# A two-layer graph-attention kernel: VectorE's order beside seven products of each head, and the rows of layer 2's logits in four column groups

## The chip, the cores and the metric

One core of a Trainium2 chip runs the whole computation in one launch. The metric is the time of an execution on the device in microseconds: 633.06 us before the change, the median of three runs (632.86 to 633.64).

## What is computed

A residual block around a graph network: `x` is 512 nodes by 768 features, with 16,896 directed edges (8192 drawn pairs in both directions, and one loop for each node). Two layers of graph attention follow one another, the first with 8 heads of 768 features each, whose outputs are concatenated, the second with one head.

```python
def gat_layer(x, W, a_s, a_d, b, edge_index, concat):
    h = (x @ W).reshape(n, H, C)
    alpha_s = einsum('nhc,hc->nh', h, a_s)
    alpha_d = einsum('nhc,hc->nh', h, a_d)
    e = leaky_relu(alpha_s[src] + alpha_d[dst], 0.2)
    ...  # softmax of e over the edges that end in one node: alpha
    out = segment_sum(h[src] * alpha[:, :, None], dst, num_segments=n)
    return out.reshape(n, H * C) + b

h = elu(gat_layer(x, W1, a_src1, a_dst1, b1, edge_index, True))    # 512 x 6144
x = layernorm(x + gat_layer(h, W2, a_src2, a_dst2, b2, edge_index, True))
```

All products are in fp32.

## The kernel before

**Stages.** The edges are turned into a dense 512x512 matrix of counts, so the attention of a head is a dense softmax and a product of a 512x512 matrix with the head's 512x768 features. Heads are worked one after the other, and three matrix products make up the work of TensorE for each head `h`: `mixed` (the attention product with the ELU that follows; it writes `gT`, the head's output, transposed), then the head's share of layer 2's product, `second` (512x768 by 768x768, added up in `h2` over the heads), then the projection of head `h + 2` (512x768 by 768x768, into `hs`). While TensorE does these, VectorE (DVE), ScalarE (ACT) and GpSimd (POOL) empty its banks, work the softmax of head `h + 1` and make the operand sums that the fast schemes below need. The loop over `h` runs for 0 to 6; head 0 and the projections of the first heads are by halves, heads 1 to 5 by thirds. Head 7 and layer 2's own attention are written out behind the loop: `last_mixed`, the last `second`, the rows of layer 2's logits, the softmax, the final product and the layernorm.

**Fast products.** By halves, a product is split 2x2 and done in 7 products instead of 8; by thirds, 512x768x768 is split into 2x3 and 3x3 blocks and done in 15 products instead of 18, named `P0` to `P14`. The left operands of some are sums of blocks (`gsums` for `second`; `in_second`, `late_` and `XB` for the projection: the X sums, L1073 and L1076), and so are the right ones (weight sums, L170: `sums` for the projection, `sums2` for `second` of the next head). Each product by thirds is 8 passes of TensorE over 256 columns (L480). It is added into one of five chains, each a bank of PSUM (the pool `mm` has five): `STEPS` gives each product its chain and the block of the output that its bank's present value is added to, or subtracted from. The next product of a chain adds to the same bank, so it must wait until the bank has been read. This reading is the product's "emptying": on DVE by L493, on ACT by L486 for the first value of a block, or on ACT with an adding DMA of POOL (L490, L491). By halves the emptyings are L447 to L451.

For the projection the order of the products is P8, P13, P9, P2, P4, P12, P6, P0, P1, P10, P5, P14, P11, P7, P3 (n = 0 to 14). P14 (n=11) and P7 (n=13) are in one chain, P11 (n=12) and P3 (n=14) in another.

**The order of each engine is written by hand.** Every engine runs its instructions in program order, and the program is a list of closures: product n is issued, then the pieces of work that a table gives to n, then the emptying of n:

```python
for n in range(15):
    pairs[n][0]()            # product n on TensorE
    ...                      # sums, logits, softmax pieces dealt to n, on DVE
    pairs[n][1]()            # emptying of n
```

What the tables deal out, as far as the change touches it: `sums3`, the operand sums of the next head's attention product (`left_sums`, L928 to L931, and `right_sums`, L939 to L942); `half_logits` and `logits` (L418, L424: a product of one tile of features with `a_s` or `a_d`, summed along the row, some 1 us each, four tiles of two for each head); `score`, `scored` and `rank` (the softmax of a tile, L640 to L662); and `sums2`.

**Weights.** `load_second(h + 1)` fetches the next head's layer-2 weights while a projection runs: SP's queue loads the rows in chunks (L145), and POOL's queue adds further blocks into some of them by DMA (`add_up`, L133). `P14`'s block is one of these: rows chunk 2, and then `add_up(B_["P14"], part(0, 1))`, 256 KB, as the second L133 into `w1r` of each head. From it and from `P4`'s block DVE makes `P6 = P14 - P4`, then `P4 = P13 + P4` in place; `P2 = P12 - P13` is made from two other loaded blocks. P2, P6 and P4 are the right operands of products 1, 6 and 3 of `second`.

**Head 0** does `second` by halves: pairs of products with emptyings `e0` and `e1`, and the softmax of head 1's tiles (`scored`) between.

**The tail.** `last_mixed` takes a table of DVE pieces, keyed by a chunk c of the product (0 to 2) and a place in it. `rows` is a bank of PSUM that collects the logits of layer 2 for all nodes in rows: `add_rows` (L1384) multiplies a stationary of 2 columns (`V`, or `al2`, each with a source and a target vector) in one of the array's column groups `j` of 32, so that the result lies on partitions 32j and 32j + 1. `rows` is cleared by a memset beforehand (L1394), copied to `row2`, and `pick` (L1416, L1418) adds the groups up by products with `picks`.

Of the kernel before, what the change touches and what calls it, by code (L numbers as in the profile page):

```python
# [37 lines left out]
def gat_pass(  # L38
# [16 lines left out]
    nc = tc.nc  # L55
    P = 128
# [365 lines left out]
    def logits(h, feats, t):  # L422
        for al, a, sign in zip(AL[h], A[h], (1.0, -1.0)):
            nc.vector.scalar_tensor_tensor(scr, feats[:, t, :], sign, a, op0=ALU.mult,  # L424
                                           op1=ALU.mult, accum_out=al[:, t:t + 1])
# [745 lines left out]
    for h in range(H - 1):  # L1171
# [14 lines left out]
        if h == 0:  # L1186
            GA, gsums = left(gT, gS)
            finish = mixed(0, AA, BB, [[besides[:1], [besides[1], sources[0]]], [[sources[1]], [sources[2]] + row],
                                       [besides[2:], list(targets)]])
            load_w1(2)()  # L1190
            load_a(2, a_src1[2], a_dst1[2])
            attend = attended(0)
            pairs = by_halves(h2, GA, B2)
            for m, _ in pairs[:2]:
                m()
            pairs[0][1]()
            for f in finish:
                f()
            gsums[0]()
            pairs[1][1]()  # L1200
            gsums[1]()
            pending[0]()
            pairs[2][0]()
            gsums[2]()
            pairs[3][0]()
            gsums[3]()
            pending[1]()
            pairs[2][1]()
            pairs[3][1]()
            fold_count(0)  # L1210
            score(0)
            for n in range(2, 7):
                (m0, e0), (m1, e1) = pairs[2 * n:2 * n + 2]
                m0()
                m1()
                if n < 6:
                    scored(n - 2)
                if n < 5:
                    score(n - 1)
                if n == 6:  # L1220
                    turn_in(0)
                    out_by_dma(2)
                e0()
                if 3 < n < 6:
                    out_by_dma(n - 4)
                if n == 6:
                    out_by_dma(3)
                    B2, sums2, load_pairs, load_first, load_rest = load_second(1)
                    load_pairs()
                    load_first()  # L1230
                    load_rest()
                e1()
                if n < 5:
                    fold_count(n - 1)
        else:
            G, gsums = g_thirds(h)

            def of_b(*names):
                return [sums2.pop(p) for p in names if p in sums2]

            amid = [[], of_b("P6", "P2"), behind] if h == 1 else [of_b("P1"), [], of_b("P4")]
            finish = mixed(h, AA, BB, [[[sources[0]], [sources[1]] + amid[0]], [row, [targets[0]] + amid[1]], [amid[2], [targets[1]]]],
                           [gsums[p] for p in ("P13", "P8")])
            behind = []
            if not last:
                load_a(h + 2, a_src1[h + 2], a_dst1[h + 2])
                attend = attended(h)
            pairs = second_by_thirds(h, G, B2)

            def sum_up(*names):  # L1250
                return [gsums[p] for p in names]

            def at(f, *args):
                return [lambda: f(*args)]

            third_sum = of_b("P3")
            plan = {0: of_b("P6") + sum_up("P14") + finish[:1], 1: finish[1:] + of_b("P4") + sum_up("P12"), 2: sum_up("P9", "P7"),
                    3: sum_up("P1") + at(score, 0), 4: sum_up("P6"), 5: at(scored, 0) + at(score, 1), 6: of_b("P1") + sum_up("P10"),
                    7: at(scored, 1) + at(score, 2), 8: sum_up("P5") + third_sum, 9: at(scored, 2) + at(score, 3),
                    10: sum_up("P11"), 11: at(scored, 3), 12: [], 13: sum_up("P3")}  # L1260
            if h > 1:
                plan[0][1:1] = [plan[13].pop()]
            if last:
                plan = {0: finish[:1], 1: finish[1:] + sum_up("P12") + at(score, 0), 2: sum_up("P9", "P7"), 3: sum_up("P1"),
                        4: sum_up("P6") + at(scored, 0) + at(score, 1), 5: sum_up("P14"), 6: sum_up("P10") + at(scored, 1) + at(score, 2),
                        7: at(out_by_dma, 0) + sum_up("P5"), 8: sum_up("P11") + at(scored, 2) + at(score, 3), 9: at(out_by_dma, 1),
                        10: at(scored, 3), 11: at(scale, 2) + sum_up("P3"), 12: third_sum + at(turn_in, 0) + at(scale, 3), 13: at(turn_in, 1)}
                AA, lsums = left_sums(H - 1, pass_.rearrange("p j n -> p (j n)"))
                plan[13] += lsums[:2]
                plan[14] = lsums[2:3]  # L1270
            behind_it = {1: of_b("P7")}

            def also(n, *what):
                plan[n] = plan.get(n, []) + list(what)

            for n, f in zip((8, 10), in_second):
                also(n, f)
            if not last:
                for f in attend:
                    also(13, f)  # L1280
            for n, (multiply, empty) in enumerate(pairs):
                if last and n > 12:
                    turn(q[n - 11], n - 11)
                multiply()
                for f in plan.get(n, []):
                    f()
                empty()
                if not last and n == 13:
                    turn_in(0)
                for f in behind_it.get(n, []):  # L1290
                    f()
                if last:
                    continue
                if n in (7, 9, 11, 14):
                    out_by_dma(min(n - 7, 6) // 2)
                if n == 5:
                    B2, sums2, load_pairs, load_first, load_rest = load_second(h + 1)
                    load_pairs()
                if n == 14:
                    rest_of_thirds()  # L1300
                    reload_x()
                    load_first()
                    load_rest()
        in_second = []
        if 0 < h and not last:
            pairs = project_by_thirds(h + 2, XB, B3)
            AA, sums3 = left_sums(h + 1)
            for n in range(15):
                pairs[n][0]()
                for p in {0: ("P6", "P2"), 1: ("P4",), 4: ("P10",), 5: ("P0",), 6: ("P1",), 9: ("P7",),  # L1310
                          12: ("P3",)}.get(n, ()):
                    sums[p]()
                if n == 5:
                    BB, rsums_ = right_sums()
                    sums3 += rsums_
                if n in (2, 3, 5, 6, 8, 9, 10):
                    for _ in range(2 if n == 8 else 1):
                        sums3.pop(0)()
                if n in (11, 13):
                    logits(h + 2, HS[h + 2], 2 + (n - 11) // 2)  # L1320
                if n in in_third:
                    in_third.pop(n)()
                if n in (12, 14):
                    sums2.pop("P2" if n == 12 else "P6")()
                pairs[n][1]()
                if n in (1, 2, 4):
                    turn_in((n + 2) // 2)
# [55 lines left out]
    def add_rows(lhsT, rhs, j, cols, start, stop):  # L1383
        nc.tensor.matmul(rows[32 * j:32 * j + 2, cols], lhsT, rhs, start=start, stop=stop,  # L1384
                         tile_position=(0, 32 * j), skip_group_check=True)
# [5 lines left out]

    first, second_, third_, fourth = (given(t) for t in range(NT))
    BB, rsums = right_sums()
    finish = last_mixed(AA, BB, [*rsums, lsums[3]], {(1, 0): [lambda: nc.vector.memset(rows, 0.0)], (2, 0): second_[:1], (2, 1): first})  # L1394
    every = slice(0, N)
    pairs = second(GA, B2)

# [2 lines left out]
            f()  # L1400

    run(pairs[0][0], pairs[0][1], pairs[1][0], pairs[1][1], *finish, gsums[0], gsums[1], pairs[2][0], pairs[2][1])
    for c in range(DC):
        add_rows(V[:, c, :], gT[:, c, :], c % 3, every, c < 3, c > 2 and c % 3 != 2)
    run(second_[1], pairs[3][0], gsums[2], pairs[3][1], *third_, pairs[4][0], *fourth, pairs[5][0], pairs[4][1], pairs[5][1], gsums[3],
        pairs[6][0])
    for t in range(NT):
        add_rows(al2[:, :, t], ident, 2, slice(t * P, (t + 1) * P), False, t == NT - 1)
    row2 = work.tile([P, N], F32, name="nr")
    nc.scalar.copy(row2, rows[:, :N])  # L1410
    fold(parts[:2])
# [114 lines left out]
```

## Time and profile before

The profiled execution took 633.37 us, 0.31 above the median; its span, from the first to the last instruction, is 631.6 us.

| | before |
|---|---|
| median of 3 runs | 633.06 us |
| profiled execution | 633.37 us |
| its span | 631.6 us |
| granted TensorE clock | 0.996 |
| TensorE (PE) busy | 620.3 us, 98% |
| TensorE's weight loads (PEld) | 483.1 us, 76% |
| VectorE (DVE) | 529.3 us, 84% |
| ScalarE (ACT) | 336.7 us, 53% |
| GpSimd (POOL) | 149.2 us, 24% |
| TensorE's share of the chain that ended last | 88% |

Weight loads run beside matmuls, and matmuls are pipelined, so a busy time is longer than the distance between starts. In lines of the timeline the columns are the start in us, the length in us, the engine, the line, the operation, output and inputs, their shapes, how many instructions are joined, and in brackets the idle time of the engine just before them with what ended it. In lines of the waits they are who waited for whom, us in total, times, and the longest.

### The profile page before, as it was taken

The numbers are of one execution on the slowest core, as the hardware profiler recorded it, in microseconds if no ns is written. First come the engines' busy times: TensorE is split into PE (matmuls) and PEld (weight loads), VectorE is DVE, ScalarE is ACT, GpSimd is POOL, SyncE is SP. The second block draws the span as 40 slices with busy tenths as digits, with TensorE's granted clock in tenths as the row PEclk, the third lists the DMA queues.
The fourth block names the chain that finished last, engine by engine and source line by source line (L and its number), as shares of the span: only waits on it lengthen the run. The fifth ranks groups of instructions, "written<-read, shape, count | busy, mean of one in ns | idle before, by whom it ended". The sixth has DMA issues, their size and how long they took to land.

```text
span 631.6 us, 8545 instructions
## 1 busy us (share of the span) xinstructions
PE 620.3 (98%) x2761; PEld 483.1 (76%) x2761; DVE 529.3 (84%) x1129; ACT 336.7 (53%) x598; POOL 149.2 (24%) x177
## 2 busy tenths in 40 slices
PE   8999999999999999999999999999999999999995
PEld 5555576556888888888888888888888888885553
DVE  8979989888898889968898778968897878968685
ACT  5875776650658236651658146751758146754361
POOL 1300011023333224323342422323342413010000
PEclk9999999999999999999999999999999999999998
DMA  8994397789999998999999998999999994590042
GB/s 292 329 245 96 70 259 249 173 244 258 246 205 152 320 253 186 181 271 222 254 214 179 310 251 182 187 290 224 226 213 202 304 279 88 124 249 2 17 76 78
DMA packets 109568, 129.45 MB, mean 205 GB/s; under 512 B 41622, under 2 KB 90446, under 8 KB 108750
## 3 DMA queue, kind: packets, MB, share of 16 engines
q1 hardware_dynamic: 75518, 91.35, 47.2%
q0 software_dynamic: 33568, 36.90, 37.7%
q10 hardware_dynamic: 432, 0.59, 0.3%
q8 instruction: 24, 0.39, 0.3%
q14 instruction: 26, 0.21, 0.1%
HBM read 99.84 MB, written 2.90 MB: 163 GB/s over the span
## 4 chain that ended last, share of the span: by engine, by line
PE 88%; DVE 5%; DMA 4%; ACT 1%; issue 1%; SPq 1%; DVEq 0%; POOLq 0%; ACTq 0%
PE mm L480 42%; PE mm L966 17%; PE mm L409 17%; PE mm L1472 3%; DMA w2r<-in_L_gnn_W_dram 3%; PE mm L1008 3%; PE held L409 2%; PE tr L742 1%; DMA w2t<-in_L_gnn_a_dst_dram 1%; PE bc L276 1%; PE held L608 1%; PE bc L742 1%; DVE h L493 0%; PE tr L1384 0%; DVE q L645 0%
## 5 line engine op out<-in xcount | busy, mean ns | idle before, releaser
L486 ACT ACTIVATE hs<-mm 128x512 f32<-128x512 f32 x30 | 17.9, 596 | 89.3 <-PE mm L480 71.2
L966 PE MATMUL mm<-PT,hs 128*128 128x256 f32 x252 | 61.3, 379 | 0.0
L493 DVE TENSOR_TENSOR hs<-hs,mm 128x512 f32<-128x512 f32 x45 | 30.8, 685 | 27.6 <-PE mm L480 27.6
L966 PEld LDWEIGHTS mm<-PT,hs 128*128 128x128 f32 x252 | 47.8, 190 | 7.2 <-ACT u L970 0.3
L649 ACT ACTIVATE q<-q,nmax 128x512 f32<-128x512 f32 x32 | 23.1, 721 | 52.9 <-DVE nmax L645 52.8
L491 POOL DMA_DIRECT2D h<-pass x22 | 26.5, 1319 | 84.4 <-ACT pass L490 75.5
L493 DVE TENSOR_TENSOR h<-h,mm 128x512 f32<-128x512 f32 x56 | 38.3, 684 | 6.2 <-PE mm L480 5.7
L966 PE MATMUL mm<-pS,gS 128*128 128x256 f32 x168 | 43.1, 379 | 0.0
L903 ACT COPY PT<-zr 128x1024 uint16<-128x1024 uint16 x34 | 39.2, 1155 | 1.5 <-DMA zr<-pS 0.9
L480 PE MATMUL mm<-w2r,gT 128*128 128x256 f32 x160 | 37.9, 385 | 0.0
L480 PE MATMUL mm<-w2r,xT 128*128 128x256 f32 x160 | 37.8, 379 | 0.0
L133 POOL DMA_DIRECT2D w1t<-in_L_gnn_W_dram x18 | 29.4, 1658 | 29.5 <-DMA w1t<-in_L_gnn_W_dram 28.7
L966 PEld LDWEIGHTS mm<-pS,gS 128*128 128x128 f32 x168 | 31.9, 190 | 4.3
L480 PE MATMUL mm<-w1t,hs 128*128 128x256 f32 x144 | 34.2, 380 | 0.5 <-DVE h L493 0.5
L480 PEld LDWEIGHTS mm<-w2r,gT 128*128 128x128 f32 x160 | 29.6, 190 | 6.6 <-DVE hs L493 3.0
L480 PE MATMUL mm<-w1r,gS 128*128 128x256 f32 x144 | 34.0, 379 | 0.0
L480 PE MATMUL mm<-w1r,hs 128*128 128x256 f32 x144 | 34.0, 379 | 0.0
L480 PEld LDWEIGHTS mm<-w2r,xT 128*128 128x128 f32 x160 | 30.4, 190 | 4.1
L970 ACT COPY u<-mm 128x256 f32<-128x256 f32 x21 | 7.8, 371 | 45.7 <-PE mm L966 45.7
L480 PEld LDWEIGHTS mm<-w1t,hs 128*128 128x128 f32 x144 | 27.2, 190 | 4.7 <-DVE h L493 0.9
L716 DVE TENSOR_SCALAR os<-nodes,idx 128x512 bf16<-128x512 f16 x104 | 29.2, 355 | 1.4 <-PE tr L742 1.4
L480 PEld LDWEIGHTS mm<-w1r,gS 128*128 128x128 f32 x144 | 27.3, 190 | 3.7
(295 smaller groups left out, 1566.6 us busy)
## 6 DMA issues: line engine op xcount, KB each, us to landing
w2r<-in_L_gnn_W_dram SPq DMA_DIRECT2D x48, 384.0 KB
w1r<-in_L_gnn_W_dram SPq DMA_DIRECT2D x43, 384.0 KB
gT<-xd SPq DMA_DIRECT2D x5, 1280.0 KB
w1t<-in_L_gnn_W_dram SPq DMA_DIRECT2D x24, 256.0 KB
h<-pass POOLq DMA_DIRECT2D x22, 256.0 KB, 4.3
w1t<-in_L_gnn_W_dram POOLq DMA_DIRECT2D x18, 256.0 KB, 6.0
w2t<-in_L_gnn_W_dram SPq DMA_DIRECT2D x15, 256.0 KB
w2t<-in_L_gnn_W_dram POOLq DMA_DIRECT2D x15, 256.0 KB, 8.9
```

The source lines that it names most:

```text
L133: nc.gpsimd.dma_start(o, i, accum_op=ALU.add)
L409: nc.tensor.matmul(ps[:, :HALF], A_[p][:, k, i * P:(i + 1) * P], B_[p][:, k, :], start=start and k == 0, stop=k == HK - 1, skip_group_chec ...
L480: nc.tensor.matmul(bank[chain][:, i * TH:(i + 1) * TH], A_[p][:, k, i * P:(i + 1) * P], B_[p][:, k, :], start=first and i == k == 0, stop= ...
L486: nc.scalar.activation(out(o), ps, AF.Copy, scale=sign)
L491: nc.gpsimd.dma_start(out(o), part, accum_op=ALU.add)
L493: nc.vector.tensor_tensor(out(o), out(o), ps, op=ALU.add if sign > 0 else ALU.subtract)
L649: nc.scalar.activation(q, q, AF.Exp, bias=nmax, scale=-1.0, accum_out=dens[t])
L716: nc.vector.tensor_scalar(o, nodes, idx[:, c:c + 1], None, op0=ALU.is_equal)
L903: nc.scalar.copy(PT.rearrange("p s n -> p (s n)").bitcast(U16).rearrange("p (s n h) -> p s n h", s=NT, h=2)[:, :, t * P:(t + 1) * P, :], p ...
L966: nc.tensor.matmul(bank[p][:, :HN], A_[p][:, k, c * P:(c + 1) * P], B_[p][:, k, :], start=over is None and k == 0, stop=k == 1, skip_group ...
L1008: nc.tensor.matmul(banks[c, p][:, :HN], A_[p][:, k, c * P:(c + 1) * P], B_[p][:, k, :], start=over is None and k == 0, stop=k == 1, skip_g ...
L1472: nc.tensor.matmul(ps[:, :cols.stop - cols.start], PT[:, s, t * P:(t + 1) * P], h2[:, s, cols], start=(s == 2), stop=(s == 1))
```

## The change

It has five parts. (1) Head 0, n=3: the emptying `e0` goes ahead of `scored(1)`. (2) `in_second`, two X sums beside `second` of head 1: from products 8 and 10 to 12 and 14. (3) The projection loop (heads 1 to 5): DVE's sums and logits are dealt to other products; P7 and P3 of the projection's weight sums one and two products earlier; the four logits of tiles 2 and 3 to n = 11, 13, 14, 14 instead of two at 11 and two at 13; of `sums2`, P2 from n=12 to n=4, P6 from n=14 to n=12, and P4 from the next attention product (`amid`) to n=14. (4) The tail: the memset of `rows` ahead of `last_mixed`, one logit from (2, 0) to (1, 1). (5) The rows: `V`'s six products of 512 columns, two in each of three groups, become four of 512 columns, one in each of four groups, and four of 256 columns, one in each; `al2`'s four products of 128 columns go to one group each instead of all to group 2. The orders of ACT, POOL and SP stay as they are.

```diff
@@ -1213,6 +1213,8 @@
                 (m0, e0), (m1, e1) = pairs[2 * n:2 * n + 2]
                 m0()
                 m1()
+                if n == 3:
+                    e0()
                 if n < 6:
                     scored(n - 2)
                 if n < 5:
@@ -1220,7 +1222,8 @@
                 if n == 6:
                     turn_in(0)
                     out_by_dma(2)
-                e0()
+                if n != 3:
+                    e0()
                 if 3 < n < 6:
                     out_by_dma(n - 4)
                 if n == 6:
@@ -1238,7 +1241,7 @@
             def of_b(*names):
                 return [sums2.pop(p) for p in names if p in sums2]
 
-            amid = [[], of_b("P6", "P2"), behind] if h == 1 else [of_b("P1"), [], of_b("P4")]
+            amid = [[], of_b("P6", "P2"), behind] if h == 1 else [of_b("P1"), [], []]
             finish = mixed(h, AA, BB, [[[sources[0]], [sources[1]] + amid[0]], [row, [targets[0]] + amid[1]], [amid[2], [targets[1]]]],
                            [gsums[p] for p in ("P13", "P8")])
             behind = []
@@ -1273,7 +1276,7 @@
             def also(n, *what):
                 plan[n] = plan.get(n, []) + list(what)
 
-            for n, f in zip((8, 10), in_second):
+            for n, f in zip((12, 14), in_second):
                 also(n, f)
             if not last:
                 for f in attend:
@@ -1305,23 +1308,23 @@
         if 0 < h and not last:
             pairs = project_by_thirds(h + 2, XB, B3)
             AA, sums3 = left_sums(h + 1)
+            some = [f for t in (2, 3) for f in half_logits(h + 2, t)]
             for n in range(15):
                 pairs[n][0]()
-                for p in {0: ("P6", "P2"), 1: ("P4",), 4: ("P10",), 5: ("P0",), 6: ("P1",), 9: ("P7",),
-                          12: ("P3",)}.get(n, ()):
+                for p in {0: ("P6", "P2"), 1: ("P4",), 4: ("P10",), 5: ("P0",), 6: ("P1",), 8: ("P7",),
+                          10: ("P3",)}.get(n, ()):
                     sums[p]()
                 if n == 5:
                     BB, rsums_ = right_sums()
                     sums3 += rsums_
-                if n in (2, 3, 5, 6, 8, 9, 10):
-                    for _ in range(2 if n == 8 else 1):
-                        sums3.pop(0)()
-                if n in (11, 13):
-                    logits(h + 2, HS[h + 2], 2 + (n - 11) // 2)
+                for _ in range({2: 1, 3: 2, 6: 1, 7: 2, 8: 1, 9: 1}.get(n, 0)):
+                    sums3.pop(0)()
+                for f in {11: some[:1], 13: some[1:2], 14: some[2:]}.get(n, ()):
+                    f()
                 if n in in_third:
                     in_third.pop(n)()
-                if n in (12, 14):
-                    sums2.pop("P2" if n == 12 else "P6")()
+                for p in {4: ("P2",), 12: ("P6",), 14: ("P4",)}.get(n, ()):
+                    sums2.pop(p)()
                 pairs[n][1]()
                 if n in (1, 2, 4):
                     turn_in((n + 2) // 2)
@@ -1391,7 +1394,7 @@
 
     first, second_, third_, fourth = (given(t) for t in range(NT))
     BB, rsums = right_sums()
-    finish = last_mixed(AA, BB, [*rsums, lsums[3]], {(1, 0): [lambda: nc.vector.memset(rows, 0.0)], (2, 0): second_[:1], (2, 1): first})
+    finish = last_mixed(AA, BB, [*rsums, lsums[3], lambda: nc.vector.memset(rows, 0.0)], {(1, 1): second_[:1], (2, 1): first})
     every = slice(0, N)
     pairs = second(GA, B2)
 
@@ -1400,12 +1403,15 @@
             f()
 
     run(pairs[0][0], pairs[0][1], pairs[1][0], pairs[1][1], *finish, gsums[0], gsums[1], pairs[2][0], pairs[2][1])
-    for c in range(DC):
-        add_rows(V[:, c, :], gT[:, c, :], c % 3, every, c < 3, c > 2 and c % 3 != 2)
+    for c in range(4):
+        add_rows(V[:, c, :], gT[:, c, :], c, every, True, False)
+    for j in range(4):
+        c, cols = 4 + j // 2, (near, far_)[j % 2]
+        add_rows(V[:, c, :], gT[:, c, cols], j, cols, False, False)
     run(second_[1], pairs[3][0], gsums[2], pairs[3][1], *third_, pairs[4][0], *fourth, pairs[5][0], pairs[4][1], pairs[5][1], gsums[3],
         pairs[6][0])
     for t in range(NT):
-        add_rows(al2[:, :, t], ident, 2, slice(t * P, (t + 1) * P), False, t == NT - 1)
+        add_rows(al2[:, :, t], ident, t, slice(t * P, (t + 1) * P), False, True)
     row2 = work.tile([P, N], F32, name="nr")
     nc.scalar.copy(row2, rows[:, :N])
     fold(parts[:2])
```

## The prediction

> **What bounds the kernel now.** I read the page's busy shares first, then the chain, then the weight-load waits of TensorE, and then the timelines of PE, DVE and POOL around each place where the diff cuts.
>
> ```profile
> span 631.6 us, 8545 instructions
> ...
> PE 620.3 (98%) x2761; PEld 483.1 (76%) x2761; DVE 529.3 (84%) x1129; ACT 336.7 (53%) x598; POOL 149.2 (24%) x177
> ...
> PE 88%; DVE 5%; DMA 4%; ACT 1%; issue 1%; SPq 1%; DVEq 0%; POOLq 0%; ACTq 0%
> ```
>
> TensorE is busy for 98% and is 88% of the chain, so the edits can only be worth the holes between its passes. The weight-load waits name who makes those holes:
>
> ```profile
> PEld mm L480 <- DVE hs L493: 3.0, 10, 0.4
> ...
> PEld mm L1008 <- DVE zr L1045: 1.1, 2, 0.7
> PEld mm L409 <- DVE h L448: 0.9, 1, 0.9
> ...
> PEld mm L480 <- DVE h L493: 0.9, 1, 0.9
> ```
>
> The columns are total, times and longest: ten waits of two per head for the emptyings of the projection (L493), two in the last attention product, one each in the two `second` stages. They are the targets. I measure a hole as the distance from one pass's start to the next, less what that pass takes when nothing holds it: 0.216 us for 128x256, 0.43 for 128x512, 0.109 for 128x128 (a product of eight 256-column passes: 1.727). After each hole the second pass follows at 0.320, not 0.216, so a hole has 0.104 beside the wait.
>
> **Part by part.** "S" is the start of a projection; product n is due to start at S + 1.727 n. The profiled execution took 633.37 (span 631.6 and 1.77 around it), 0.31 above the median 633.06; sums are made on 633.37.
>
> *Head 0.* At 114.96 TensorE waited 0.486 + 0.103 for the emptying L448, which stood on DVE behind a softmax step (L662, L640, L645) and ran from 115.16. Emptied first, it is early: -0.59. What stands behind it, the rank of a tile, feeds ACT, which is 53% busy.
>
> *Head 1, `second`.* At 193.48 the hole is 0.626 + 0.104: DVE ran the two X sums (L1076 at 189.00, 0.69; L1073 at 192.99, 0.69) and only then the emptying L493 at 193.59. Moved to products 12 and 14, they lie after it. I leave 0.05 because `gsums["P3"]` then ends at 197.07 against a start of its product at 197.15: -0.68.
>
> *P4 out of the attention product, heads 2 to 5 and the last.* One 0.60 us addition leaves the stretch before L982. L982 then waits for TensorE anyway, so only 0.05 of each ~0.16 hole goes: five times -0.05, -0.25 (bounds 0 and -0.84, all of the holes).
>
> *The projection, heads 1 to 5.* This is the large term. What is there, for head 3 (S = 340.45):
>
> ```profile
> 360.43 0.96 DVE L424 SCALAR_TENSOR_TENSOR scr<-hs,a_s 128x768 bf16<-128x768 f32 x1
> ...
> 361.43 0.96 DVE L424 SCALAR_TENSOR_TENSOR scr<-hs,a_d 128x768 bf16<-128x768 f32 x1
> ...
> 362.31 0.68 DVE L493 TENSOR_TENSOR hs<-hs,mm 128x512 f32<-128x512 f32 x1
> ...
> 364.11 0.68 DVE L493 TENSOR_TENSOR hs<-hs,mm 128x512 f32<-128x512 f32 x1
> ...
> 367.19 0.68 DVE L170 TENSOR_TENSOR w1t<-w1r 128x512 f32<-128x512 f32 x1
> ```
>
> ```profile
> 363.05 1.59 PEld L480 LDWEIGHTS mm<-w2r,gT 128*128 128x128 f32 x8 [0.38 <-DVE hs L493]
> 364.85 1.59 PEld L480 LDWEIGHTS mm<-w2r,gT 128*128 128x128 f32 x8 [0.21 <-DVE hs L493]
> ```
>
> Two logits ahead of the emptying of product 11, then two additions ahead of that of product 12: P7 (n=13) and P3 (n=14) start late by 0.326, 0.329, 0.326, 0.331 and 0.325 with their refills, 1.64 in all. The change takes one logit and two additions away from there: by the durations above (additions 0.60 apart, logits 0.96), emptying 11 ends at S+21.7, in time. That is the gain.
>
> But P6 of the layer-2 weight sums, the line at 367.19 (`w1t<-w1r`), moves from n=14 to n=12 and ahead of emptying 12. It is P14 - P4, and P14's block is finished by an adding DMA of POOL (L133, 256 KB), so it cannot start before that lands:
>
> ```profile
> 358.95 1.19 POOL L133 DMA_DIRECT2D w1r<-in_L_gnn_W_dram  x1 [0.57 <-DMA w1r<-in_L_gnn_W_dram]
> ```
>
> The tile's view puts 4.9 us from this issue to landing, so 363.81, or S+23.36. Before, P6 at S+26.7 came 3.4 us after it and nobody saw it. Now VectorE reaches P6 at S+21.6. The five adds are issued at 218.81, 290.21, 358.95, 429.57 and 501.00 and take 4.9, 4.5, 4.9, 4.4 and 4.3:
>
> ```profile
> DMA to landing us min/median/max: 4.5/4.5/4.5
> ```
>
> (head 2). Landings after S: 24.10, 24.74, 23.36, 23.10 and 23.99; mean 23.86. Queued behind the waiting P6 on DVE is emptying 12, which frees the bank that product 14 adds into: with 0.60 for P6 and 0.68 for the emptying TensorE can start product 14 at landing + 1.40, and it is due at S+24.19. Stalls: 1.385 (head 1, with 0.07 for issues a little later), 1.955, 0.575, 0.315 and 1.205: 5.44, with five refills 5.96. Net of the 1.64 gained: **+4.32**. What follows does not add to it: emptying 13, two logits, P4 and emptying 14 end at landing + 5.3, and L976 of the next attention product, which had 0.80 of idle ahead of it, is due at landing + 5.1 to 5.2 and TensorE needs what it leads to only some products later. Bounds: with every landing as early as head 4's the term is +0.5, with every one as late as head 2's +8.7, with none late -1.64. I take the measured ones, because POOL's and SP's orders do not change and what holds those adds, the weight rows ahead of them on busy DMA engines (nine tenths or more in most of these slices), doesn't either. P2, moved to n=4, needs DMAs issued in `second`; it hides in VectorE's slack there (8.1 to 8.8 after S, emptying due at 8.9): 0.
>
> [...]
>
> *The tail's fillers.* TensorE lost 0.456 + 0.104 at 563.70 and 0.146 + 0.104 at 570.30:
>
> ```profile
> 563.52 0.48 DVE L1394 MEMSET tr<- 128x512 f32 x1
> 563.91 0.41 DVE L1045 TENSOR_TENSOR zr<-mm,w 128x256 f32<-128x256 f32 x1
> ...
> 569.31 0.95 DVE L1388 SCALAR_TENSOR_TENSOR scr<-h,w2t 128x768 bf16<-128x768 f32 x1
> ...
> 570.19 0.42 DVE L1045 TENSOR_TENSOR zr<-mm,w 128x256 f32<-128x256 f32 x1
> ```
>
> Both fillers leave the place before L1045: -0.81. The memset now delays the first L1036 (557.28) by some 0.3, and the pass that waits for L1039 is due at 558.74 with L1039 at 558.6 to 558.8: +0.05 (bounds 0 and +0.2). -0.76.
>
> *The rows.*
>
> ```profile
> 577.53 1.89 PE L1384 MATMUL tr<-gT,V 128*2 128x512 f32 x12
> ...
> 587.29 1.04 PE L1384 MATMUL tr<-ident,al 128*2 128x128 f32 x8
> ```
>
> The 12 passes start in threes (577.530, .537, .544), so three column groups run abreast: four rounds of 0.43, 1.72. Afterwards two rounds of 512 and two of 256: 1.29, **-0.43**. The eight passes of `al`, all in one group, come 0.109 apart, 0.87; in four groups two rounds, 0.22: **-0.65**. The copy for the pick (588.36 to 588.95, its product at 589.65) keeps its cover. That four groups run abreast is seen at L742 (bf16, four starts each 0.215). Bounds: these, and 0 if fp32 passes in the fourth group queue.
>
> [...]
>
> Sum: -0.59 - 0.68 - 0.25 + 4.32 - 0.76 - 0.43 - 0.65 = **+0.96**: 634.33 for the profiled run, 634.0 on the median.
>
> **Rivals.** *No landing is late* (B). Then the projection gives its 1.64 and the whole -5.0: 628.1. For it speaks no row of this trace. Against it: five of five adds landed 0.3 to 1.9 us beyond the last harmless time (S+22.8). [...] *The adds land somewhat earlier* (C): stalls of TensorE leave the DMA engines time, which could bring later heads' loads forward; all as head 4's gives -2.9, 630.2. Below a mean landing of S+23.4 the kernel is measurably faster. *The adds land late* (D), the slower side: each 0.1 us in the mean landing costs 0.5 us in all. Two of the five are already at S+24.1 or beyond, and head 2's in all five would give 634.0 + 4.4 = 638.4. From a mean of S+23.9, which is almost the measured one, the kernel is slower by over 0.2% (1.27 us, about what a measurement of this kernel can tell from no change). *The rows gain nothing* (E): fp32 passes in a fourth group take turns; 635.1.
>
> **How the numbers follow.** The sum, with a scatter of half a microsecond in the mean landing (the five have 0.6 between them): 0.62, on both sides of the line at 634.33. B 0.09, C 0.09, D 0.14, E 0.06. Split by the line: faster takes B, C and 0.05 of the sum's scatter; same 0.31, all from the sum; slower D, E and the sum's remaining 0.26. Range: the early and late means S+23.3 and S+24.4, 631.2 and 636.7; I round to 631.0 and 637.0 for the rows and the memset, and leave out B, part of C and of D.
>
> **What would show it.** In the changed trace VectorE should sit idle ahead of `w1t<-w1r` at S+21.6 in all five projections until the second L133 of POOL has landed, and TensorE should show one hole of 0.4 to 2.1 us before product 14 and none before product 13. The holes at 114.96, 193.48, 563.70 and 570.30 are gone, `tr<-gT,V` shows fours, and the al rows two rounds. I am wrong if P6 starts at once, if the landings move by more than half a microsecond, or if a later stage gives the tail's 1.8 us back.

## The result, and the profile after

| | before | changed |
|---|---|---|
| median | 633.16 us | 637.77 us |
| ratio to before (95% interval) | 1 | 1.0067 (1.005 to 1.0083) |
| executions of the comparison | 632.86 to 633.86 | 633.89 to 639.16 |
| profiled execution, its span | 633.37, 631.6 us | 637.83, 636.0 us |
| granted TensorE clock | 0.996 | 0.994 |

The change makes the kernel slower, by about 4.2 us as the ratio goes and 4.6 between the medians. It also makes it restless: its executions spread over 5 us, where the kernel before keeps within 1. One more execution of the changed kernel, at a granted clock of 0.849, took 723.6 us and is left out of the ratio and of the spread.

The page after, the same rows as before:

```profile
span 636.0 us, 8555 instructions
...
PE 619.0 (97%) x2765; PEld 484.4 (76%) x2765; DVE 529.3 (83%) x1129; ACT 336.4 (53%) x598; POOL 149.4 (23%) x177
...
PE 82%; DMA 12%; DVE 2%; issue 1%; ACT 1%; SPq 0%; POOL 0%; ACTq 0%; POOLq 0%; DVEq 0%
```

DMA has gone from 4% to 12% of the chain. The waits of the weight loads, and then those of VectorE, name the place:

```profile
PEld mm L480 <- DVE hs L493: 8.8, 6, 2.6
```

```profile
DVE w1t L170 <- DMA w1r<-in_L_gnn_W_dram: 12.7, 5, 3.6
```

Ten waits of TensorE for a projection's emptying, 3.0 us together, have become six with 8.8. VectorE, which never waited for this DMA before, waits for it five times, 12.7 us. In DVE's timeline for head 1, P6 is the first line and emptying 12, queued behind it, the second:

```profile
223.85 0.69 DVE L170 TENSOR_TENSOR w1t<-w1r 128x512 f32<-128x512 f32 x1 [3.60 <-DMA w1r<-in_L_gnn_W_dram]
224.46 0.68 DVE L493 TENSOR_TENSOR hs<-hs,mm 128x512 f32<-128x512 f32 x1
```

TensorE at the same time: product 13, the late product 14, and the first passes of the attention product.

```profile
221.09 1.89 PE L480 MATMUL mm<-w2r,gT 128*128 128x256 f32 x8
225.20 3.13 PE L480 MATMUL mm<-w2r,gT 128*128 128x256 f32 x8 [2.22 <-DVE hs L493]
228.12 1.62 PE L966 MATMUL mm<-PT,hs 128*128 128x256 f32 x4
```

Two things are to be seen. Product 14 starts 2.38 us after it was due, and its eight passes take 3.13 us instead of 1.89. By the windows (stretch, its length, busy times, granted clock, DMA share, GB/s) the passes are slow because the granted clock was halved, some 0.7 us after work had begun again:

```profile
225.20:225.80 0.60, 0.60 (x3) 0.55 (x4) 0.60 (x1) 0.00 (x0) 0.00 (x0) 1.00 1.20 191
225.80:227.00 1.20, 1.20 (x5) 0.95 (x4) 1.20 (x4) 0.00 (x0) 0.00 (x0) 0.54 1.25 197
227.00:229.00 2.00, 2.00 (x7) 1.53 (x6) 1.97 (x5) 0.60 (x1) 0.00 (x0) 0.50 0.37 57
```

From 225.99 to 229.36 passes come 0.427 apart instead of 0.216; against full speed this loses 1.65 us, 1.69 with the pass in which the clock changed.

Head 1 has a second new hole, 0.76 and its refill before product 6. ScalarE waited there for the transposed attention weights of head 2, its first emptying and all of VectorE's work behind that came late, and P2, now at n=4, stood ahead of emptying 4 (ACT's timeline, then DVE's):

```profile
199.25 1.17 ACT L903 COPY PT<-zr 128x1024 uint16<-128x1024 uint16 x1 [2.48 <-DMA zr<-pS]
```

```profile
207.55 0.69 DVE L170 TENSOR_TENSOR w1t<-w1t 128x512 f32<-128x512 f32 x1
208.15 0.68 DVE L493 TENSOR_TENSOR hs<-hs,mm 128x512 f32<-128x512 f32 x1
```

The gains of the change are there too. The fillers and the rows of the tail:

```profile
563.13 0.48 DVE L1397 MEMSET tr<- 128x512 f32 x1
563.52 0.41 DVE L1036 TENSOR_TENSOR u<-u,mm 128x256 f32<-128x256 f32 x1
```

```profile
582.74 1.47 PE L1387 MATMUL tr<-gT,V 128*2 128x512 f32 x16
...
592.08 0.40 PE L1387 MATMUL tr<-ident,al 128*2 128x128 f32 x8
```

The memset is ahead of the first L1036 and costs a hole of 0.047 later; the holes at 563.70 and 570.30 of before are gone. From the start of V's rows to the next product it is 1.40 us (1.82 before), from al's 0.33 (0.97 before).

Holes between passes, profile before against profile after, make up the difference:

| place | forecast | profile after |
|---|---|---|
| head 0, emptying L448 | -0.59 | -0.59 |
| head 1, X sums | -0.68 | -0.67 |
| P4 out of the attention products | -0.25 | -0.25 |
| holes before products 13 and 14 of before | -1.64 | -1.64 |
| new holes before product 14, with refills | +5.96 | +7.14 |
| half-speed passes in head 1 | none | +1.69 |
| hole before product 6 in head 1's projection | none | +0.86 |
| tail's fillers | -0.76 | -0.76 |
| rows of the logits | -1.08 | -1.06 |
| sum | +0.96 | +4.72 |

The spans differ by 4.4: the first 15 us, which the change leaves alone, ran 0.6 quicker in the profile after, and the stretch behind TensorE's last pass took 0.3 longer.

### The profile page after: what moved, and what is told of

Read it like the earlier page. It is cut to its first block, busy times and chain, and to the rows that moved or that the text cites. A ratio compares the mean times of both kernels' runs of the same rounds, so it can differ in the third digit from the quotient of the medians.

```text
span 636.0 us, 8555 instructions
## 1 busy us (share of the span) xinstructions
PE 619.0 (97%) x2765; PEld 484.4 (76%) x2765; DVE 529.3 (83%) x1129; ACT 336.4 (53%) x598; POOL 149.4 (23%) x177
## 4 chain that ended last, share of the span: by engine, by line
PE 82%; DMA 12%; DVE 2%; issue 1%; ACT 1%; SPq 0%; POOL 0%; ACTq 0%; POOLq 0%; DVEq 0%
PE mm L480 32%; PE mm L966 20%; PE mm L409 19%; DMA w1r<-in_L_gnn_W_dram 12%; PE mm L1478 3%; PE mm L1008 3%; PE held L409 2%; PE tr L742 1%; DVE hs L493 1%; DMA hs<-in_x_dram 1%; PE held L608 1%; PE bc L742 1%; SPq L145 0%; ACT os L714 0%; PE mm L307 0%
## 5 line engine op out<-in xcount | busy, mean ns | idle before, releaser
L649 ACT ACTIVATE q<-q,nmax 128x512 f32<-128x512 f32 x32 | 23.1, 721 | 51.2 <-DVE nmax L645 50.9
L480 PE MATMUL mm<-w2r,gT 128*128 128x256 f32 x160 | 39.5, 391 | 5.8 <-DVE hs L493 5.8
L480 PEld LDWEIGHTS mm<-w1r,hs 128*128 128x128 f32 x144 | 27.2, 190 | 3.8 <-DVE hs L1127 0.2
```

Of the source, the lines that this page charges most:

```text
L480: nc.tensor.matmul(bank[chain][:, i * TH:(i + 1) * TH], A_[p][:, k, i * P:(i + 1) * P], B_[p][:, k, :], start=first and i == k == 0, stop= ...
L649: nc.scalar.activation(q, q, AF.Exp, bias=nmax, scale=-1.0, accum_out=dens[t])
```

## The experiments

The theory: P6's wait for the landing of P14's adding DMA, with emptying 12 queued behind it, costs all of the loss, part of it through the clock. Its rival: the redealt sums and logits hold up the emptyings themselves.

### P6 back at n=14

```diff
-for p in {4: ("P2",), 12: ("P6",), 14: ("P4",)}.get(n, ()):
+for p in {4: ("P2",), 14: ("P6",)}.get(n, ()):
...
-amid = ... else [of_b("P1"), [], []]
+amid = ... else [of_b("P1"), [], of_b("P4")]
```

> The changed kernel with P6 of layer 2's weight sums back at n=14 and P4 back in the next attention product; all else as changed. Theory (P6's wait for the landing of P14's adding DMA costs the time, with the half-speed passes that follow its longest wait): the holes before product 14 (2.38, 1.33, 0.76, 0.68, 1.48 and five refills) and the half-speed passes (1.7) go, the gains of the other parts stay, and only the new hole at product 5 of head 1's projection (0.86) is left: 633.1 - 5.0 + 0.86 = 629.0. Rival (the redealt sums and logits themselves hold up the emptyings, and the wait is only what ends last): holes before products 13 or 14 stay, 633 or more.

Measured: 629.55 us (628.43 to 630.78), ratio to before 0.9942 (0.9929 to 0.9956). The profiled execution is the fastest, 628.43. Around product 14 of head 3, DVE first (emptying 12, then P6 with no wait), then TensorE:

```profile
360.62 0.69 DVE L493 TENSOR_TENSOR hs<-hs,mm 128x512 f32<-128x512 f32 x1 [1.04 <-PE mm L480]
...
364.83 0.69 DVE L170 TENSOR_TENSOR w1t<-w1r 128x512 f32<-128x512 f32 x1
```

```profile
360.42 3.62 PE L480 MATMUL mm<-w2r,gT 128*128 128x256 f32 x16
```

Products 13 and 14 run as one row of 16 passes, without a hole. The rest of the redealt order is harmless and worth what was forecast: the terms without the new holes give -0.59 - 0.67 - 1.64 - 0.76 - 1.06 = -4.72, so 628.7 against 628.43. The rival falls. The hole before product 6 is not there in this profile, so the 0.86 expected for it did not come.

### P14's add ahead of P1's

```diff
-            load_rows(1)
-            add_up(B_["P1"], part(1, 2))
             load_rows(2)
             add_up(B_["P14"], part(0, 1))
+            load_rows(1)
+            add_up(B_["P1"], part(1, 2))
```

> The changed kernel, but load_rest fetches rows chunk 2 and adds into P14's block before rows chunk 1 and P1's add: P6 stays at n=12, what it waits for comes earlier by the distance of the two adds (1.7 to 2.8 us in the changed trace). Theory: holes before product 14 shrink to about 0.5 in head 1 and nothing elsewhere, no half-speed passes: about 629.6. Rival (the landing is bound by the DMA engines' backlog, not by the order): landings shift by under 0.5 us and the time stays above 635. Second rival: P6 no longer waits but something else in that place does (P1's block, used in the attention product, comes late): over 631 with a new hole in the attention product.

Measured: 628.67 us (628.14 to 630.55), ratio 0.9928 (0.9914 to 0.9941), 0.9 below the time expected. P6 stays at n=12; only its data come earlier. Holes before product 14: 0.32 in head 1, 0.07 in head 5, none elsewhere, no half-speed passes. So it is the landing and not the place of P6. The second rival has a share: P1's sum, made in place in the attention product, waited for another add of POOL that reads P1's block (0.83 us of TensorE in head 6):

```profile
514.97 0.69 DVE L170 TENSOR_TENSOR w1r<-w1t,w1r 128x512 f32<-128x512 f32 x1 [2.05 <-DMA w1t<-w1r]
```

### All parts but the projection loop's, and one move of it alone

The third kernel is the one before with head 0's, head 1's and the tail's edits as in the diff. The fourth is the one before with this alone:

```diff
-if n in (12, 14):
-    sums2.pop("P2" if n == 12 else "P6")()
+for p in {4: ("P2",), 12: ("P6",), 14: ("P4",)}.get(n, ()):
+    sums2.pop(p)()
...
-amid = ... else [of_b("P1"), [], of_b("P4")]
+amid = ... else [of_b("P1"), [], []]
```

> The kernel before with all parts but the projection loop's and P4's: head 0's emptying, the two X sums of head 1, the tail's fillers, the rows in four groups. By the holes of the trace of before: -0.59 - 0.68 - 0.76 - 1.08 = -3.1, so 630.0. Rival (a stage behind takes part of it back, the pick or the softmax of layer 2 above all): 631.5 or more.

> The kernel before with one move alone: P2 of sums2 to n=4, P6 to n=12, P4 to n=14 of the projection. Theory (landing): five waits of VectorE ahead of P6 and holes before product 14 as in the changed kernel, half-speed passes after the longest, the old hole before product 13 stays: 633.1 + 6.6 + 0.5 + 1.7 + 0.9 - 0.9 - 0.25 = 641.6, 639 to 643 as the landings fall. Rival (redealt sums and logits): within 1 us of the kernel before.

Measured: 630.37 us, ratio 0.9953 (0.9939 to 0.9967), for the small parts: their forecast gain of 3.1, less 0.3. And 638.77 us (637.98 to 640.59), ratio 1.0082 (1.0066 to 1.0097), for the weight sums alone: holes of 1.80, 2.58, 0.37, 0.08 and 1.19 before product 14, with half-speed passes behind the 2.58 only (1.64 lost). Three moved additions carry the loss; the expected 641.6 was 2.8 too high for the median and 1.0 for the profiled execution (640.59), whose holes are 6.0 and not the 6.62 of the first profile after, and which has none before product 6.

### A later landing, and TensorE kept busy in it

```diff
             add_up(B_["P1"], part(1, 2))
             load_rows(2)
-            add_up(B_["P14"], part(0, 1))
             add_up(B_["P0"], B_["P12"])
             load_four("P11", "P10")
+            add_up(B_["P14"], part(0, 1))
```

```diff
+                if n == 14:
+                    idle = tr.tile([P, 512], F32, name="tr")
+                    for _ in range(15):
+                        nc.tensor.matmul(idle[:, :P], ident, ident, start=True, stop=True)
                 pairs[n][0]()
```

> The changed kernel, but the add into P14's block is issued two places later on POOL's queue, behind the adds of P0 and P11 (about 2 us later). Theory of the wait: every hole before product 14 grows by about 2 us, to 2.7 to 4.4, 10 us in all. Theory of the clock (TensorE's passes run at half speed for some 1.7 us after a hole of over 2 us, as behind the 2.38 of head 1 and not behind 1.48 in the changed trace): all five holes are followed by half-speed passes, so 637.8 + 10 + 4 x 1.7 = 654.6. Rival (the half-speed passes of head 1 came by chance and have nothing to do with the hole): one or no such stretch, 648.

> The kernel with the late add into P14's block (663.4), with 15 products of the identity with itself (30 passes of 128 columns, 3.3 us) put on TensorE ahead of product 14 in each of the five projections; their result is read by nobody. Theory (the half-speed passes, 10.5 us beyond full speed in that run's trace, follow from TensorE's idleness in the hole): holes are filled to under 1.8 us in heads 1 to 4 and their stretches go, only head 5's hole (7.7) may keep one: 663.4 - 8.5 = 655. Rival (something else brings them, the DMA traffic or the point of time): stretches stay, 663.

Measured: 663.44 us with the late add, more than expected, since the holes are 4.38, 4.77, 3.42, 3.77 and 7.72 (24.1 in all, not 17). All five are followed by half-speed passes, which lose 2.48, 3.10, 1.64, 1.65 and 1.60: 10.5 us. With 3.3 us of useless products in each hole: 655.11 us. TensorE's timeline in head 1, late add first, then with the products:

```profile
221.14 1.89 PE L480 MATMUL mm<-w2r,gT 128*128 128x256 f32 x8
227.24 3.78 PE L480 MATMUL mm<-w2r,gT 128*128 128x256 f32 x8 [4.22 <-DVE hs L493]
```

```profile
221.92 3.51 PE L1316 MATMUL tr<-ident 128*128 128x128 f32 x30
226.17 1.99 PE L480 MATMUL mm<-w2r,gT 128*128 128x256 f32 x8 [0.73 <-DVE hs L493]
```

The landing is as late as it was, and yet product 14 takes 1.99 instead of 3.78. With idle stretches of 0.90, 1.92, 0.50 and 0.99 heads 1 to 4 have no half-speed passes; head 5, with 3.29 idle, still has them (granted clock 0.55 from 526.8 to 530.6). So it was TensorE's idleness that halved its clock here, and work that nobody needs saved 8.3 us (663.44 to 655.11).

### The order without the wait, in two forms

```diff
 first form: P6 back at n=14, P2 at n=9, P4 behind chunk 1 of the attention product
+for p in {9: ("P2",), 14: ("P6",)}.get(n, ()):
+amid = ... else [of_b("P1"), of_b("P4"), []]
 second form: P14's add first, P6 at n=13, P2 at n=9, P1's sum behind chunk 1
+for p in {9: ("P2",), 13: ("P6",), 14: ("P4",)}.get(n, ()):
+amid = ... else [[], of_b("P1"), []]
```

> The changed kernel with P6 back at n=14, P2 at n=9, and P4 of the next head behind chunk 1 of the attention product (beside a logit) and not ahead of L982 in chunk 2. Theory: as with P6 back alone, and the 0.06 ahead of the last passes of five attention products goes as well: 629.55 - 0.3 = 629.2, no hole before products 13 and 14. Rival (VectorE is late at chunk 2's first addition instead, since a logit and P4 stand ahead of it): new holes in the attention product, 629.6 or more.

> The changed kernel with P14's add ahead of P1's, P6 at n=13, P2 at n=9, and P1's sum one chunk later in the attention product (it waited 2.05 us for POOL's add that reads P1's block in the run with P14's add first, head 6, and TensorE lost 0.83 there). Theory: no hole before product 14 nor in the attention product, 628.67 - 0.32 - 0.07 - 0.83 - refills 0.3 = 627.2 by that profile, 628 by the median. Rival (moved to chunk 1's end, P1's sum only delays chunk 2): 628.7 or more.

Measured: 627.90 us (627.83 to 628.90), ratio 0.9921 (0.9907 to 0.9934), and 628.57 us (627.83 to 628.97), ratio 0.9924 (0.9911 to 0.9938). Both beat both kernels, and the measurement does not tell them apart. The profiled executions are the fastest, 627.83, and neither has a hole in the projections; the 0.06 ahead of the last passes of the attention products is gone as well. The first form came out 1.3 below the 629.2 expected, and why is not shown; the second came out 0.6 above the 628 expected of its median.

### The changed kernel once more

> The changed kernel once more, for a second profile. Theory: what differs from one execution to the next is when DMAs land: the holes before product 14 vary by head within about 1 us, and the hole at product 6 of head 1's projection (0.76 in the first profile, behind a transposing DMA that landed 2.5 us after ScalarE was ready for it) comes and goes; 634 to 639. Rival (the holes are fixed by the orders of the engines): the same five holes within 0.2 us, and the hole at product 6 again.

Measured: 635.71 us (632.22 to 637.5, eight executions), ratio 1.004 (1.0028 to 1.0052). The profiled one took 632.22, with holes before product 14 of 0.38, 0.64, 1.18, none and 1.25, no half-speed passes and no hole before product 6. The median lies in the expected 634 to 639, and the profiled execution below it. By the terms of the table: -0.59 - 0.67 - 0.25 - 1.64 - 0.76 - 1.06 + 3.44 + four refills of 0.104 = -1.1, so 632.3. The two profiles of one program differ by 5.6 us, and landings explain that within 0.3: 3.2 us in the holes, 0.1 in a refill, 1.7 in the clock that the longest hole halved, and 0.9 before product 6, where a transposing DMA was late.

Head 1's adding DMA scatters most, and mostly before it is issued. POOL's lines, the first profile after and then this one:

```profile
219.03 1.19 POOL L133 DMA_DIRECT2D w1r<-in_L_gnn_W_dram  x1 [0.70 <-DMA w1r<-in_L_gnn_W_dram]
```

```profile
216.99 1.19 POOL L133 DMA_DIRECT2D w1r<-in_L_gnn_W_dram  x1 [0.96 <-DMA w1r<-in_L_gnn_W_dram]
```

With S at 197.77 and 198.19 the issues are at S+21.3 and S+18.8, 2.5 us apart, both behind a wait of POOL for weight rows; from issue to landing it then takes 4.7 and 4.3. Why the rows came late is not shown.

### P2 at n=4, and P6 behind emptying 12

```diff
 the first form of above, with P2 as in the changed kernel
-for p in {9: ("P2",), 14: ("P6",)}.get(n, ()):
+for p in {4: ("P2",), 14: ("P6",)}.get(n, ()):
```

```diff
 the changed kernel, with P6 behind emptying 12
-for p in {4: ("P2",), 12: ("P6",), 14: ("P4",)}.get(n, ()):
+for p in {4: ("P2",), 14: ("P4",)}.get(n, ()):
     sums2.pop(p)()
 pairs[n][1]()
+if n == 12:
+    sums2.pop("P6")()
```

> The best version so far (P6 back at n=14, P4 behind chunk 1) with one difference: P2 at n=4, as in the changed kernel, and not at n=9. Theory (P2 ahead of emptying 4 costs only when ScalarE's first emptying is late behind the transposing DMA of head 2's weights): the fastest runs equal those with P2 at n=9 (627.8), others are up to 0.9 slower; median 628.4. Rival (P2's place is free of cost, as forecast): the same distribution, 627.9. Second rival (always paid): all runs 0.9 higher.

> The changed kernel with P6 still at n=12, but behind emptying 12 and not ahead of it. VectorE waits for the same landing at nearly the same moment. Theory (the wait costs only by the emptying queued behind it): product 14 starts in time, no half-speed passes; what now stands behind the wait is emptying 13 and two logits, and the attention product may lose 0 to 0.6 for each head: 629 to 631.5. Rival (a wait of VectorE for a DMA costs what it lasts, wherever it stands): 634 to 639 as the changed kernel.

P2 at n=4: 628.72 us (628.10 to 631.00), ratio 0.9929 (0.9914 to 0.9943). The price of P2's place is seen in the profile, not in the times. ScalarE waited 1.98 us there for the transposing DMA, VectorE for ScalarE's first emptying, and P2 then stands ahead of an emptying that is already late (0.25 us of TensorE). With P2 at n=9 ScalarE's wait was 1.57 and there was no hole. But the 631.0 of this profile is mostly head 6's P1 sum, which waited 3.40 us for POOL's add and cost TensorE 2.18; so the medians, whose intervals overlap, don't price P2.

P6 behind emptying 12: 630.70 us (628.77 to 633.29), ratio 0.9961 (0.9941 to 0.9981). VectorE's wait in head 2 and TensorE beside it:

```profile
292.70 0.69 DVE L170 TENSOR_TENSOR w1t<-w1r 128x512 f32<-128x512 f32 x1 [1.57 <-DMA w1r<-in_L_gnn_W_dram]
```

```profile
290.24 3.62 PE L480 MATMUL mm<-w2r,gT 128*128 128x256 f32 x16
```

VectorE still waits for the landing, in four heads and 3.6 us in all (it comes to P6 later, since emptying 12 has to wait for product 12's end), and products 13 and 14 run through. With the wait still there, one line moved by one place turns the loss into a gain of 2.6 us. What is queued behind the wait now is emptying 13 and the logits, and these cost something in the attention product (holes of 0.25 and 0.25 in head 3, 0.13 and 0.24 in head 6), as expected; head 6 has 0.78 more from P1's sum, as in the run with P14's add first.

## Why the prediction was wrong, point by point

**The mechanism was right.** P6 moved ahead of a landing, VectorE waited for it in all five projections, emptying 12 stood behind it, product 14 started at landing + 1.4, and there is nothing before product 13. Rival B, that no landing is late, is out: even the quicker of the changed kernel's two profiles has four late ones. Rival E, that the rows gain nothing, is out too.

**The step that failed is the size of "+4.32".** In the first profile after, the same term is 7.14 + 1.69 - 1.64 = 7.19. Of the 2.87 missing, 1.69 are half-speed passes, for which the forecast had no term at all, and 1.18 are later landings. With the landings alone the sum would have been +2.14, or 635.5, inside the range. The rest of the miss is P2's "0", below.

**Head 1's hole cost more than itself and its refill of 0.104.** The forecast let every pass after a hole run at full speed. The hole of 2.38 us halved the clock for 3.4 us and cost 1.69 more. The terms of the two bounds, "+0.5" to "+8.7", lacked it too: in these runs holes of up to 2.18 us left the clock alone and those of 2.38 us and more halved it, so a hole of 1.96, as head 2's landing gives, lies below both, and a scatter of half a microsecond beyond it lies above both.

In the profiles before and after, the starts of the stretches of one granted clock lie whole multiples of 3.413 us apart: 5.92 and 627.14 in the one, 182 of them apart, 4.04, 225.90, 229.32 and 632.09 in the other, 65, 1 and 118 apart (the last of each lies behind TensorE's last pass). Head 1's halved stretch, 225.90 to 229.32, lasts one of them. What separates the cases in these runs is the length of the hole: 2.38 us or more halved the clock each of eight times, 2.18 or less never did. Where between the two it turns, and whether the hole's place has a part in it, is not shown.

**The five landings** were taken from one execution as if they were the kernel's. Product 14's holes in us:

| head | forecast | first profile after | second profile after |
|---|---|---|---|
| 1 | 1.39 | 2.38 | 0.38 |
| 2 | 1.96 | 1.33 | 0.64 |
| 3 | 0.58 | 0.76 | 1.18 |
| 4 | 0.32 | 0.68 | 0 |
| 5 | 1.21 | 1.48 | 1.25 |
| sum | 5.44 | 6.62 | 3.44 |

The landings were not fixed: head 1's lies at S+26.0 in one execution, where the hole at product 6 had delayed the stage by 0.86 already, at S+23.1 in the other, and at S+24.1 before the change. That POOL's and SP's orders do not change did not hold the adds in place, as the prediction argued: its own sign of being wrong, landings that move by more than half a microsecond, came up in heads 1 and 2 of both profiles. The mean moved less, to S+24.2 and S+23.4 against 23.86, which is within the half microsecond that the range allowed. Part of the miss is thus luck: the median of the second set of executions, 635.71, lies inside the stated range, and that of the first, 637.77, 0.8 outside.

**"P2 ... hides in VectorE's slack: 0"** rested on 0.1 us of slack ahead of emptying 4, worked out for head 3 and taken for head 1, where an X sum stands in the same stretch and ScalarE can be late behind a transposing DMA (2.48 us in the first profile after). The hole there cost 0.86 in one profile and nothing in the other. P2's own addition is 0.60 of it from start to start; without it some 0.16 of hole would have been left, an estimate from these rows.

**The small terms** stand within 0.05 each, the rows at 1.06 of 1.08. V's passes start in fours, the first four within 0.02 us (582.738 to 582.758), and al's eight in two rounds 0.109 us apart.

**The rivals.** D, late landings, had the right sign and, at 638.4, nearly the right time, but in part by luck: its sum has 9.8 us of holes where 6.62 were measured, and the half-speed passes and the hole before product 6, which it didn't have, made up most of the rest. In the first profile after, the mean landing was S+24.1 once the 0.86 of head 1 is taken off, past the point of S+23.9 named for it; in the second it was S+23.4.

## What to carry to other kernels

When work is moved ahead of a DMA that it needs, the landing in one profile is a sample: look at the same landing in several heads and executions, and at what holds its issue, and put the wait behind whatever frees a bank or a buffer for the engine that bounds. VectorE's wait cost here what was queued behind it, not what it lasted: one place in the order decided between 637.8 (635.7 in the second set of executions) and 630.7. And price a hole in TensorE twice, once as idle time and, where it comes near or above the 2.38 us that halved the clock here, once more as a stretch at half clock (it lost 1.6 us or more in these runs).

## What the runs showed of the hardware

- Holes of 0.08 to 2.18 us left the clock alone; those of 2.38, 2.58, 3.29 and above (eight in all) were always followed by passes at half speed, starting between 0 and 1.2 us after work began again; they lasted 3.4 us in the profile after (225.99 to 229.36) and 6.1 in head 2 of the run with the late add (304.5 to 310.6). Dummy products in the hole prevented it in four heads of five; in the fifth 3.29 us of idleness were left.
- The same 256 KB adding DMA landed up to 2.9 us apart, against the start of the stage, from one execution of the changed kernel to the next; 2.5 of this were there when it was issued.
- fp32 passes in four column groups ran abreast: eight of 128 columns took 0.33 us up to the next product's start, 0.97 when in one group.
- A DMA chain that was covered came up in three of the faster kernels: the in-place sum of P1 waited 2.05 us (P14's add first), 3.40 (P2 at n=4) and 2.0 (P6 behind emptying 12) for an add that reads its block; the profiles before and after have no such wait.
